# A fused perceiver layer: the order of the attention units, the place of the state-space stage, and silu written with exp and ln

## The chip, the cores and the metric

The kernel runs on one core of a Trainium2 chip. The metric is the device time of one execution in microseconds. Engines are named as in the profile: PE is TensorE, ACT is ScalarE, DVE is VectorE, POOL is GpSimd, SP is SyncE, whose queue issues nearly all DMAs.

## The reference

Inputs are 512 query rows `x` and 8192 context rows `ctx`, each of width 512. All arithmetic is float32. Three blocks follow one another, each added to `x`:

```
q, k, v = LN(x) Wq + bq, ctx Wk + bk, ctx Wv + bv        # 16 heads of 64
x += softmax(q k^T / 8) v Wo + bo                        # cross-attention

h = LN(x); r = rms(h) * norm1
xin, z = split(r in_proj^T)                              # 1024 channels each
xin = silu(causal_conv4(xin) + conv_b)
dt, B, C = split(xin x_proj^T)                           # 32, 16, 16
delta = softplus(dt dt_proj^T + dt_b)
s[t] = exp(delta[t] A) * s[t-1] + delta[t] xin[t] B[t]   # 16 states per channel
y = (sum over states s C + xin D) * silu(z)
u = h + y out_proj^T
x += u + (silu(rms(u) w1) * (rms(u) w3)) w2

h = LN(x); top 2 of 16 experts, sigmoid gates
x += gated experts(h) + shared expert(h)                 # silu(gate) * up, down
```

The recurrence runs over the 512 rows in order, so the second 256 rows need the states that the first 256 leave, and nothing of the first 256 depends on the second after attention.

## The kernel before

Every float32 matmul operand is split into a float16 high and a float16 low part, and a product is made of three float16 matmuls. Attention works on pairs of heads (8 pairs, `p`) and on halves of the 512 queries (`h`). A unit is one pair and one half: 32 steps (`NSTEP`), each over 256 of the 8192 context rows.

A step's `scores` (L345) runs eight score matmuls of 256 columns (L359, L360) into two PSUM tiles. ACT then takes the exponential twice, in float32 (L367, two instructions) and in float16 (L369, two instructions); in every second step (`m % 2 == 1`) DVE casts instead (L371). DVE subtracts the two to get the low part (L372). `av` (L375) multiplies by the values one step later: eight matmuls of 130 columns (value low, a zero, value high, a one, L389) and eight of 65 (L392), into one bank for each head of the pair. `unit_end` (L393) divides by the sums, transposes, adds the bias and stores a high and a low part in `oT` (L414, L415).

The maxima, keys and values come from `filler` (L421), a generator of PE work. One pass projects keys and values of two pairs over 16 context chunks (L250 to L252, L274 to L276) and takes each query's maximum (`smax_units`, L297, L302, L310). There are four passes (`NPASS`). Keys and values go to DRAM (`k_d`, `v_d`); `main_load` (L333) brings 1.3 MB for every four steps back through SP. Queries are placed by `qplace` into one of four pairs of tiles, 6 DMAs per pair; the row of maxima (`maxrow_units`) is written into the same tile.

The order on PE is the program's own in attention (`manual_schedule`); all other orders are a planner's. Units run pair by pair, both halves of a pair in turn:

```python
units = [(p, h) for p in range(NPAIR) for h in range(2)]      # L543
NFILL = 12 * NSTEP - 4                                        # L560
rate = (NPASS - 1) * PASSN / NFILL                            # L561
```

Pass 0 runs by itself; passes 1 to 3 are spread evenly over the first 12 units by `advance`, twice in each step. `weight_prep` (L509) splits the later weights, one yield in every second step. Units 12 to 14 have no filler. Unit 15 (loop at L605) takes two yields of `tail` per step: the output projection of the first 256 rows (`wo_proj(0)`), `prep(0)` and `delta(0, 0)`.

`tail` (L630) holds the rest. `prep(s)` (L764) does norms, in-projection, convolution, silu (ACT's Silu, L795, L796), x-projection, and broadcasts B and C from DRAM to 128 partitions (`load_bc`, L856). `delta(s, q)` (L866) makes softplus and `silu(z)` (L890) for two of eight channel blocks. `scan(s, b)` (L896) goes through four chunks of four states: four exponentials on ACT (L906), a product (L909), the scan (L913) and a product (L916) on DVE, and sums over states on PE with the identity as weight (L919). Three buffers `dAs` and `hss` rotate. After attention a loop over eight (s, q) (L1050) runs the scans, with `prep(1)` between those of the first half, and `outproj(0)` and the MLP of the first half (`ffn`, L952) between those of the second. `lnexp` (L655) loads the ACT table that holds exp and ln after each Silu. Then come `outproj(1)`, the MLP of the second half, router, shared expert and 18 expert rounds (`moe`, L1256).

Of the kernel before, what the change touches and what calls it, by code (L numbers as in the profile page):

```python
# [37 lines left out]
def perceiver_layer(ctx: ExitStack, tc: tile.TileContext, a: dict, out: bass.AP):  # L38
# [8 lines left out]
    oT = const.tile([P, 2, NPAIR, NQ], F16, name="oT", tag="big16")  # L47
    oTh, oTl = oT[:, 0], oT[:, 1]
# [5 lines left out]
    ]  # L54
    k_d = [[scr.tile([P, 2, 2 * CH], F16, name=f"k_d{p}_{c}") for c in range(NDC)] for p in range(NPAIR)]
# [90 lines left out]
    NQT = 4  # L146
    qlms = []
    qhhs = [(L if i == (NPAIR - 1) % NQT else sb1).tile([P, 2, NQ], F16, name=f"qhh{i}") for i in range(NQT)]
    for i in range(NQT):
        t = (L if i == (NPAIR - 1) % NQT else sb1).tile([P, 2, NQ], F16, name=f"qlm{i}")  # L150
        nc.gpsimd.memset(t[64:128], 0.0)
        qlms.append(t)
# [60 lines left out]
    def qplace(p, qh, ql):  # L213
        qhh = qhhs[p % NQT]
        qlm = qlms[p % NQT]
        for hh in range(2):
            s = slice(hh * 64, hh * 64 + 64)
            nc.sync.dma_start(qhh[0:64, hh, :], qh[s])
            nc.sync.dma_start(qhh[64:128, hh, :], qh[s])
            nc.sync.dma_start(qlm[0:64, hh, :], ql[s])  # L220
        state[p]["q"] = qhh, qlm
# [91 lines left out]
    def maxrow_units(p, runm):  # L313
        qlm = state[p]["q"][1]
# [9 lines left out]
        for hh in range(2):  # L324
            nc.sync.dma_start(
                qlm[64:65, hh, :].rearrange("o (a b) -> o a b", b=P), r[hh * 4 : hh * 4 + 4, :]
            )
# [17 lines left out]
    def scores(u, m, ld, sp, alone=False):  # L345
# [3 lines left out]
        qhh, qlm = state[p]["q"]  # L349
        qs = slice(h * HQ, (h + 1) * HQ)  # L350
        pss = []
        for i in range(2):
# [5 lines left out]
            for hh in range(2):  # L358
                nc.tensor.matmul(ps[:, hh], lhsT=k[:, hh, sl], rhs=qhh[:, hh, qs], start=True, stop=False)  # L359
                nc.tensor.matmul(ps[:, hh], lhsT=b[:, hh, sl], rhs=qlm[:, hh, qs], start=False, stop=True)  # L360
# [4 lines left out]
        cast = m % 2 == 1  # L365
# [9 lines left out]
    def av(po, m, x):  # L375

        v, ph, pl = x
        kw = dict(skip_group_check=True)
        for x in range(2):
# [14 lines left out]
    def unit_end(u, po, sp):  # L394
        p, h = u
        oq = sp.tile([P, 2, 2, 64], F32, name="oq", tag="oq", bufs=1)
        rl = sp.tile([P, 2, 2], F32, name="rl", tag="rl", bufs=1)
        for hh in range(2):
            nc.scalar.copy(oq[:, :, hh, :], po[hh][:, :, 0:64])
        for hh in range(2):  # L400
            nc.vector.reciprocal(rl[:, hh], po[hh][:, :, VW - 1])
            nc.vector.tensor_tensor(oq[:, :, hh, :], po[hh][:, :, 65:129], oq[:, :, hh, :], ALU.add)  # L402
        for hh in range(2):
            nc.vector.tensor_tensor(
                oq[:, :, hh, :], oq[:, :, hh, :], rl[:, hh].unsqueeze(2).to_broadcast((P, 2, 64)), ALU.mult
            )
# [5 lines left out]
        qs = slice(h * HQ, (h + 1) * HQ)  # L412
        ptf = pt.rearrange("d q n -> d (q n)")
        nc.scalar.activation(oTh[:, p, qs], ptf, AF.Identity, bias=bv)  # L414
        nc.vector.scalar_tensor_tensor(oTl[:, p, qs], ptf, bv, oTh[:, p, qs], ALU.add, ALU.subtract)  # L415
# [5 lines left out]
    def filler():  # L421
# [22 lines left out]
        mr, nw = [], None  # L444
        for g in range(NPASS):
# [8 lines left out]
            else:  # L454
                wk, wv, wq = nw
                qh = [qproj(p, w) for p, w in zip(pr, wq)]
                yield 2 * 2592
            runm = [sb2.tile([P, 4, 2, CH], F16, name=f"runm{i}", tag=f"runm{i}", bufs=1) for i in range(2)] if g else None
            ks = [[None] * NCH for _ in pr]
            for c in range(NCH):  # L460
# [11 lines left out]
                for n, gen in enumerate(gens):  # L472
# [5 lines left out]
                    if mr and c == 0:  # L478
                        yield from mr.pop(0)
# [29 lines left out]
    def weight_prep():  # L509
# [10 lines left out]
        def fetch(j):  # L520
            f = sb2.tile([P, 1024], F32, name="mpf", bufs=2)
# [3 lines left out]
        nf = fetch(0)  # L525
        yield
        for j, (name, i, dst) in enumerate(blocks):
            f = nf
            if j + 1 < len(blocks):
                nf = fetch(j + 1)  # L530
# [44 lines left out]
    for n in range(NLAST * NSTEP):  # L575
        u, m = units[n // NSTEP], n % NSTEP
        if m == 0:
            assert state[u[0]].get("ready"), u
# [780 lines left out]
```

## Time and profile before

| what | value |
|---|---|
| median of 3 runs | 2650.54 us (2645.51 to 2652.3) |
| the profiled execution | 2653.45 us, span 2651.7 us |
| PE, DVE, ACT busy | 2410.6, 2049.4, 1955.5 us (91, 77, 74% of the span) |
| first step of units 0, 12, 13, 14, 15 | 278.5, 1650.9, 1703.1, 1755.2, 1809.8 us |
| last AV matmul of attention | 1914 us |
| first and last scan (L913) | 1918, 2263 us |
| first expert's matmul (L1222) | 2449 us |
| DMA | 531 MB, mean 200 GB/s |

The page cuts the span in 40 slices of 66 us; each digit is the busy share of a slice in tenths:

```profile
PE   7999998999999899998999998998878688998895
DVE  6876688877877877777877777997899999633785
ACT  5787787888787788867788887997868476432784
```

Slices 5 to 25 are attention beside the passes, 26 to 29 attention alone and with the preparation, 30 to 34 the scans, then MLP and experts. A duration in the profile includes latency that overlaps the next instruction, so the distance between starts is what an engine gives for one instruction. PE durations are modelled.

### The profile page before, as it was taken

Reading aid. Unit: us, or ns where it says so; the run is one execution under the profiler, and the core shown is the slowest. Engines: PE = TensorE matmul, PEld = TensorE weight load, DVE = VectorE, ACT = ScalarE, POOL = GpSimd, SP = SyncE. Lnnn points to the kernel's source line nnn. Section 1 sums busy time; section 2 is a strip of 40 time slices with the busy share of each in tenths; the row PEclk is TensorE's granted clock in tenths of the full one; section 3 lists DMA queues with packets and bytes.
Section 4 is the critical chain, followed back from the end, with each engine's and each line's share of the span. In section 5 each row is a group of like instructions: output and inputs, shape, how many; then the busy total and the mean of one; then the engine's idle time right before and its main releaser. Section 6 shows DMA issues by size and latency. Waiting matters only on the chain. (4 is left out here: it accounts for less than half of the span.)

```text
span 2651.7 us, 54346 instructions
## 1 busy us (share of the span) xinstructions
PE 2410.6 (91%) x21806; PEld 1693.5 (64%) x21806; DVE 2049.4 (77%) x2403; ACT 1955.5 (74%) x3734; POOL 44.2 (2%) x58
## 2 busy tenths in 40 slices
PE   7999998999999899998999998998878688998895
PEld 4454676777666677766677766997656466665442
DVE  6876688877877877777877777997899999633785
ACT  5787787888787788867788887997868476432784
POOL 2000000000000000000000000000000000001001
PEclk9999999999899999989999998999989889999998
DMA  7973899866598866658966655887511322675896
GB/s 265 308 255 128 268 284 270 242 169 187 166 268 264 265 189 176 184 152 250 253 176 190 173 162 129 201 204 206 171 56 41 96 72 82 229 233 200 294 337 222
DMA packets 353686, 531.42 MB, mean 200 GB/s; under 512 B 25106, under 2 KB 218834, under 8 KB 353300
## 3 DMA queue, kind: packets, MB, share of 16 engines
q1 hardware_dynamic: 352148, 523.69, 65.6%
q0 software_dynamic: 1280, 4.20, 0.5%
q8 instruction: 173, 2.83, 0.5%
q14 instruction: 85, 0.70, 0.1%
HBM read 397.68 MB, written 126.94 MB: 198 GB/s over the span
## 5 line engine op out<-in xcount | busy, mean ns | idle before, releaser
L372 DVE TENSOR_TENSOR phl<-p,phl 128x1024 f16<-128x1024 f32 x512 | 625.9, 1224 | 175.0 <-ACT phl L369 158.9
L367 ACT ACTIVATE p<-pss 128x512 f32<-128x512 f32 x1024 | 596.8, 619 | 126.1 <-PE pss L360 50.7
L302 ACT ACTIVATE sf<-psx 128x512 f16<-128x512 f32 x1024 | 557.7, 622 | 79.1 <-PE psx L297 77.2
L359 PE MATMUL pss<-qhh,k 128*128 128x256 f16 x2048 | 486.2, 277 | 18.5 <-ACT phl L369 18.0
L360 PE MATMUL pss<-qlm,kb 128*128 128x256 f16 x2048 | 485.2, 276 | 0.6 <-DMA kb<-k_d 0.4
L389 PE MATMUL po<-v,phl 128*128 128x130 f16 x4096 | 327.2, 222 | 5.2 <-DVE oq L402 4.7
L310 DVE TENSOR_TENSOR runm<-runm,sf 128x2048 f16<-128x2048 f16 x240 | 292.4, 1218 | 45.7 <-ACT sf L302 45.2
L389 PEld LDWEIGHTS <-phl 128*128 128x128 f16 x4096 | 273.9, 99 | 69.4 <-issue 21.5
L369 ACT ACTIVATE phl<-pss 128x512 f16<-128x512 f32 x512 | 312.3, 610 | 0.0
L274 PE MATMUL psv<-wh_v,ctxc 128*128 128x256 f16 x1024 | 283.4, 277 | 7.7 <-DVE khl L258 3.4
L275 PE MATMUL psv<-wl_v,ctxc 128*128 128x256 f16 x1024 | 282.2, 276 | 1.2 <-DVE wl_v L176 1.2
L276 PE MATMUL psv<-wh_v,ctxc 128*128 128x256 f16 x1024 | 282.1, 276 | 0.0
L359 PEld LDWEIGHTS <-k 128*128 128x128 f16 x2048 | 202.2, 99 | 63.7 <-issue 18.0
L360 PEld LDWEIGHTS <-kb 128*128 128x128 f16 x2048 | 202.7, 99 | 61.0 <-issue 22.2
L297 PE MATMUL psx<-khl,qh 64*128 64x512 f16 x1024 | 212.5, 395 | 21.3 <-ACT sf L302 18.4
L371 DVE CAST phl<-p 128x1024 f16<-128x1024 f32 x256 | 176.1, 688 | 58.1 <-ACT p L367 57.7
L392 PE MATMUL po<-v,phl 128*128 128x65 f16 x4096 | 209.9, 194 | 9.3 <-DVE phl L372 9.3
L250 PE MATMUL psk<-ctxc,wh_k 128*128 128x512 f16 x512 | 198.6, 388 | 21.1 <-DVE vs L281 10.5
L919 PE MATMUL py<-hs,ident 128*128 128x256 f32 x512 | 148.1, 447 | 67.1 <-DVE hs L916 67.0
L251 PE MATMUL psk<-ctxc,wh_k 128*128 128x512 f16 x512 | 197.2, 385 | 0.7 <-DVE ctxc L234 0.7
L252 PE MATMUL psk<-ctxc,wl_k 128*128 128x512 f16 x512 | 196.8, 384 | 0.0
L392 PEld LDWEIGHTS <-phl 128*128 128x128 f16 x4096 | 172.8, 98 | 12.8 <-DVE phl L372 12.0
(304 smaller groups left out, 3711.9 us busy)
## 6 DMA issues: line engine op xcount, KB each, us to landing
v<-v_d SPq DMA_DIRECT2D x128, 520.0 KB, 4.4
k<-k_d SPq DMA_DIRECT2D x256, 256.0 KB, 5.8
ctxc<-ctx_d SPq DMA_DIRECT2D x96, 512.0 KB, 5.2
wef<-in_gu_dram SPq DMA_DIRECT2D x72, 512.0 KB, 5.9
v_d<-vs SPq DMA_DIRECT2D x128, 260.0 KB, 3.8
k_d<-khl SPq DMA_DIRECT2D x128, 256.0 KB, 4.2
kb<-k_d SPq DMA_DIRECT2D x128, 256.0 KB, 5.4
wpm<-w_d SPq DMA_DIRECT2D x48, 512.0 KB, 3.9
```

The costliest lines, as they stand in the source:

```text
L274: nc.tensor.matmul(ps[:, t, :], lhsT=ct[i // 2][:, 0, i % 2, sl], rhs=wh[:, i, :], start=i == 0, stop=False)
L275: nc.tensor.matmul(ps[:, t, :], lhsT=ct[i // 2][:, 0, i % 2, sl], rhs=wl[:, i, :], start=False, stop=False)
L276: nc.tensor.matmul(ps[:, t, :], lhsT=ct[i // 2][:, 1, i % 2, sl], rhs=wh[:, i, :], start=False, stop=i == NC4 - 1)
L302: nc.scalar.activation(dst, ps, AF.Copy, scale=1.0 / (8.0 * WS))
L310: nc.vector.tensor_tensor(r, r, sf, ALU.max)
L359: nc.tensor.matmul(ps[:, hh], lhsT=k[:, hh, sl], rhs=qhh[:, hh, qs], start=True, stop=False)
L360: nc.tensor.matmul(ps[:, hh], lhsT=b[:, hh, sl], rhs=qlm[:, hh, qs], start=False, stop=True)
L367: nc.scalar.activation(p32[:, i], pss[i], AF.Exp, scale=sc)
L369: nc.scalar.activation(ph[:, i], pss[i], AF.Exp, scale=sc)
L372: nc.vector.tensor_tensor(pl, p32, ph, ALU.subtract)
L389: nc.tensor.matmul(o, lhsT=ph[:, i, hh, qs], rhs=vv, start=first, stop=False, **kw)
L392: nc.tensor.matmul(o, lhsT=pl[:, i, hh, qs], rhs=vv_, start=False, stop=last, **kw)
```

## The change

1. Units go through all eight pairs with the first half of the queries, then through all with the second. The three later passes lie beside the first 6 units (192 steps, `NPREP`), and `weight_prep` advances at every step with a third load buffer. Queries go to DRAM (`q_d`), together with the row of maxima, and `qload` brings a unit's half in three DMAs into one of two tile pairs, up to four steps ahead.
2. From step 192 (unit 6) on, all values of a unit go into one PSUM bank: `av` issues per head, tile and query block three matmuls of 65, 64 and 65 columns. The freed bank holds the output projection and `py`.
3. From step 194 on `tail` is advanced in the attention loop; it yields the number of steps until its next turn. The output projection takes each pair as its unit ends (`ended`); `prep(0)`, then `delta(0, q)` and `scan(0, b)` lie beside units 8 to 14. Two `dAs` and `hss` there, four later. A cast on DVE in every fourth step for units 8 to 15 (`casts`).
4. Silu outside the last stages is `x * exp(-ln(1 + exp(-x)))`: `sigmoid` gives three ACT passes, DVE multiplies. The MLP of the first half (`exps=True`) does so too.
5. After attention: `wo_proj(1)`, `prep(1)` with `outproj(0)` and two MLP blocks between, then delta and scans of the second half with an MLP block after each scan.

```diff
-    units = [(p, h) for p in range(NPAIR) for h in range(2)]
+    units = [(p, h) for h in range(2) for p in range(NPAIR)]
+    NPREP = 2 * (NPASS - 1) * NSTEP
-    NFILL = 12 * NSTEP - 4
+    NFILL = NPREP - 4
...
+    for n in range(NU * NSTEP):
+        j, m = n // NSTEP, n % NSTEP
...
+        if n == NPREP:
+            while pend:
+                drain()
+            finish()
...
+            half = tail(tc, a, out, const, scr, ident, x_sb, mlp_d, oTs, y_d, xd_d, (ps_s, ps_o, ps_x, bank_j), ended)
+            turn = n + 2
...
+        cur = scores(u, m, loads[n // 4], sp, n > NFILL, 2 if j < NPAIR else 4)
+        advance(start + LEAD + (n + 0.5) * rate)
+        if m == 4:
+            finish()
+        while half and n >= turn:
+            d = next(half)
+            if d is None:
+                turn = NU * NSTEP
+            else:
+                turn = max(turn, n) + d
...
+        if m >= NSTEP - 4 and j + 1 < NU:
+            p, h = units[j + 1]
+            if state[p].get("ready") and ("q", h) not in state[p]:
+                qload(j + 1, units[j + 1])

-        cast = m % 2 == 1
+        cast = m % casts == 1

+        if len(po) == 1:
...
+                        nc.tensor.matmul(o, lhsT=ph[:, i, hh, qs], rhs=vh1, start=first, stop=False, **kw)
+                        nc.tensor.matmul(o[:, 0:64], lhsT=ph[:, i, hh, qs], rhs=vl, start=False, stop=False, **kw)
+                        nc.tensor.matmul(o, lhsT=pl[:, i, hh, qs], rhs=vh1, start=False, stop=last, **kw)

+    def qload(j, u):
+        p, h = u
+        qs = slice(h * HQ, (h + 1) * HQ)
+        qhh, qlm = qts[j % 2]
+        nc.sync.dma_start(qhh[0:64], q_d[p][0:64, 0, :, qs])
+        nc.sync.dma_start(qhh[64:128], q_d[p][0:64, 0, :, qs])
+        nc.sync.dma_start(qlm[0:65], q_d[p][0:65, 1, :, qs])
+        state[p]["q", h] = qhh, qlm

+    def sigmoid(src, scale, bias=None):
+        t = m2.tile([P, 2, H], F32, name="sig", tag="w2k", bufs=4)
+        for j in range(2):
+            kw = {} if bias is None else dict(bias=bias[:, j : j + 1])
+            if bias is not None:
+                nc.scalar.activation(t[:, j], src[:, j], AF.Exp, scale=-scale, **kw)
+            elif j == 0:
+                nc.scalar.activation(t, src, AF.Exp, scale=-scale)
+        nc.scalar.activation(t, t, AF.Ln, bias=one)
+        nc.scalar.activation(t, t, AF.Exp, scale=-1.0)
+        return t

     def scan(s, b):
-            dlu[s, q].append(ps_s.tile([P, 2, H], F32, name="py", tag="pss"))
+            pp, tag = (ps_s, "pss") if s else (ps_o, "po1")
+            dlu[s, q].append(pp.tile([P, 2, H], F32, name="py", tag=tag))
...
+            yield 3
             for n in range(4):
                 k = nq * 4 + n
                 nc.tensor.matmul(py[:, j, :], lhsT=ident, rhs=hs[:, n, 1:], start=k == 0, stop=False)
+            if nq < 3:
+                yield 2

+    yield 44
+    yield from wo_proj(0)
+    yield from prep(0)
+    yT0 = None
+    for q in range(4):
+        yield from delta(0, q)
...
+        for j in range(2):
+            yield from scan(0, 2 * q + j)
+        gate(0, q, yT0)
+    yield None
```

The yields of `prep(0)` sum to 35 steps, of `delta` to 5, of `scan` to 20. In all, `tail` before attention's end takes steps 194 to 480 of 512.

## The prediction

> **What bounds the kernel now.** I read the page first: PE is busy for 91% of the span, DVE for 77%, ACT for 74%, an average over stages with different limits. So I cut the span where the step starts (every fourth score matmul, L359) and the first scan (L913) show a change of stage, and asked for the busy time of each engine in each stretch (columns: stretch and its length, then busy us and instructions of PE, PEld, DVE, ACT, POOL, the granted clock, DMA share, GB/s).
>
> ```profile
> 0.00:278.50 278.50, 254.71 (x1550) 135.34 (x1551) 197.44 (x231) 199.21 (x366) 19.50 (x25) 0.95 0.71 238
> 278.50:1650.90 1372.40, 1313.01 (x13410) 945.14 (x13409) 1059.96 (x1267) 1104.53 (x2160) 2.29 (x6) 0.97 0.73 210
> 1655.00:1808.00 153.00, 149.41 (x2259) 139.33 (x2258) 146.19 (x163) 144.13 (x290) 0.00 (x0) 1.00 0.82 203
> 1809.80:1914.00 104.20, 86.79 (x977) 71.01 (x974) 80.08 (x131) 83.73 (x164) 0.53 (x1) 0.95 0.69 196
> 1914.00:2080.00 166.00, 129.30 (x624) 96.48 (x625) 157.70 (x148) 116.86 (x278) 0.37 (x5) 0.90 0.15 48
> 2080.00:2270.00 190.00, 147.84 (x801) 111.03 (x799) 181.66 (x161) 107.95 (x227) 4.78 (x5) 0.93 0.27 85
> 2270.00:2452.00 182.00, 164.63 (x1201) 112.73 (x1199) 75.28 (x149) 64.15 (x88) 8.46 (x8) 0.95 0.69 235
> 2452.00:2651.70 199.70, 159.44 (x922) 77.64 (x920) 145.43 (x153) 130.61 (x159) 8.22 (x8) 0.94 0.80 284
> ```
>
> The rows are: pass 0; units 0 to 11 beside passes 1 to 3; units 12 to 14 alone; unit 15 beside the preparation of the first half; the scans of the first half; those of the second; the MLP with router and shared expert; the experts and the end. PE bounds rows 2 and 3 (96% and 98%), DVE bounds rows 5 and 6 (95% and 96%). In row 3 all three engines are nearly full, so attention has no engine to lend. In rows 5 and 6 PE is busy under 80% and ACT 60 to 70%.
>
> A busy time overlaps its neighbour's, so costs must come from starts. The timeline of PE in unit 13, columns start, length, what:
>
> ```profile
> 1732.32 0.27 PE L360 MATMUL pss<-qlm,kb 128*128 128x256 f16 x1
> 1732.42 0.62 PE L389 MATMUL po<-v,phl 128*128 128x130 f16 x8
> 1732.88 0.40 PE L392 MATMUL po<-v,phl 128*128 128x65 f16 x8
> 1733.13 0.27 PE L359 MATMUL pss<-qhh,k 128*128 128x256 f16 x1
> ```
>
> Eight 130-column matmuls take 0.46 us from start to start (57 ns each), eight of 65 columns 0.25 (30 each), a score matmul 109. A step is 8 x 109 + 8 x (57 + 30) ns = 1.57 us; units 12 and 13 took 52.2 and 52.1 us, 1.63 a step. The same view of ACT there, and of DVE in the scans:
>
> ```profile
> 1731.16 0.59 ACT L369 ACTIVATE phl<-pss 128x512 f16<-128x512 f32 x1
> 1731.63 0.60 ACT L367 ACTIVATE p<-pss 128x512 f32<-128x512 f32 x1
> 1732.11 0.62 ACT L369 ACTIVATE phl<-pss 128x512 f16<-128x512 f32 x1
> ```
>
> ```profile
> 1984.33 2.29 DVE L913 TENSOR_TENSOR_SCAN hs<-dA,hs 128x1028 f32<-128x1028 f32 x1
> 1986.54 1.20 DVE L909 TENSOR_TENSOR hs<-bc,du 128x1024 f32<-128x1024 f32 x1
> 1987.65 1.22 DVE L916 TENSOR_TENSOR hs<-hs,bc 128x1024 f32<-128x1024 f32 x1
> 1988.79 2.29 DVE L913 TENSOR_TENSOR_SCAN hs<-dA,hs 128x1028 f32<-128x1028 f32 x1
> ```
>
> So ACT needs 0.477 us per exponential of 512, DVE 2.21 per scan and 1.13 per product of 1024 (L372 has that size: 1.14); its cast L371 is 0.72 behind the next start. A step with a cast in every second one costs ACT 3 x 0.477 = 1.43, DVE 1.14 + 0.36 = 1.50.
>
> **The change part by part. Units 0 to 5 beside the passes.** The passes' work now lies beside 192 steps instead of 384. Row 2 is bound by PE, so the stage loses what 192 steps take on PE: 192 x 1.57 / 0.975 (granted clock) = 309 us; I take 307. The rest, 1065 us, is projections and maxima. ACT needs 768 evacuations of maxima x 0.478 + 192 of projections at some 0.53 + 192 x 1.43 = 744 of these 1065, DVE 192 maxima x 1.13 + 192 evacuations at 0.63 + 104 weight splits at 0.94 + 192 x 1.50 = 724. Neither comes near. Weight preparation runs at every step: its 52 loads and 104 stores stay hidden as now (DMA share 0.73; attention's loads of 1.3 MB per 4 steps are halved in number, so the rate stays at some 210 GB/s). The queries go through DRAM, three loads per unit on SP; the next unit's are issued up to four steps (20 us) ahead, so I cost them at nothing; uncovered, they cost a landing of about 5 us at each of 16 units. Unit 6 starts at 278.5 + 1065 = 1343.5.
>
> **Units 6 and 7.** Alone but for the first output projection, which takes 42 matmuls of 216 ns there = 9.1 us on a full PE, and the emptying of the pipeline at the pool change (unit 14 took 54.6 against 52.1): 104.3 + 9.1 + 2.5 = 116.
>
> The new AV order splits 130 columns into 65 + 64: 24 small matmuls per step for 8 + 8. A rule speaks against this: the Trainium skill, TensorE: Matmul & The Clock Gate, section Back-to-back issue gap, gives about 81 ns sustained for a stream of weight load and matmul pairs at 128 columns. By it 24 pairs cost 1.94 us, 1.25 more per step, 80 us in these two units alone. The row L392 is exactly such a stream, with a weight load before each, at 30 ns; by it the cost is 0.72 against 0.70. I take the row, from 0 to +0.1 us per step.
>
> **Units 8 to 15, the state-space part beside them.** The program spends 9 steps until the projection is done, 35 on the preparation, 4 x 45 on delta and scans, and 32 steps are left. With a cast in every fourth step, ACT costs (8 + 6) x 0.477 / 4 = 1.67 a step, DVE 1.14 + 0.18 = 1.32, PE 1.57.
> - 9 steps: 15 us.
> - Preparation. Added on DVE: convolution 32 instructions, 24 x 0.40 + 8 x 0.26 = 11.7; norms, gates and splits some 16. On ACT: per pair of blocks a copy 0.48, three halo and split copies 0.7, sigmoid 2 x 0.36 + 2 x 0.52; with the norms 20. On PE 14.8. ACT 58.4 + 20 = 78.5, DVE 74, PE 73: three nearly equal loads. Row 4 is the nearest: 104 us with 83.7 on its busiest by union. But it holds table loads that are removed (below). I take 85.
> - Scans, per 45 steps: DVE 45 x 1.32 + 8 chunks x 4.48 (a scan, two products) + 4.2 for delta and gate + 1.3 for unit ends = 100.8. ACT 75.2 + 14.2 (32 exponentials of 256 at 0.40, carries) + 4.8 + 0.5 = 94.7. PE 70.6 + 32 x 0.218 + 3.2 = 81, at the clock of row 5 some 88. So DVE bounds it: 403 for four. Row 5 ran at 95% of DVE: 403 / 0.96 = 420. Bounds: 403, and 485 at the 83% that row 4 made of PE.
> - 32 steps at 1.67: 53.5.
>
> Sum 15 + 85 + 420 + 53.5 = 573.5; attention's end at 1343.5 + 116 + 573.5 = 2033.
>
> Moved queues: the eight broadcast loads of 512 KB stand on SP ahead of the next chunk's k. At 284 GB/s (last row) 4.2 MB take 15 us against 9 for four steps: up to 6 us, once, inside the range. The store before them waits for ACT's xd, with those loads behind it; k is loaded a chunk ahead. POOL only clears tiles. The AV of a unit's first step waits for DVE's reading of the old sums, now behind a scan of 2.2 us; while DVE bounds the stage this costs nothing.
>
> **Silu by exp and ln.** Row 4's ACT groups and waits:
>
> ```profile
> L795 ACT ACT_TABLE_LOAD x2 | 2.6, 1283 | 0.0
> ...
> L367 ACT ACT_TABLE_LOAD x1 | 1.3, 1283 | 0.0
> ```
>
> ```profile
> PE pss L359 <- ACT phl L369: 10.6, 6, 4.3
> ```
>
> Eleven loads in that stretch, 14.1 us, and PE waits up to 4.3 us for ACT. The Trainium skill (ScalarE: Activation LUTs, What ACT_TABLE_LOAD costs) adds a drain of 1.38 us, 2.66 per switch. The row speaks against it: the next instruction starts 1.29 us after the load's start (median of L656). Kept beside attention, four gates with two switches each would cost ACT 10.3 us by the row, 21 by the rule. The new form costs two more passes of 0.52 each. In the later stages ACT is not the bound, and the saved loads are worth nothing.
>
> **After attention.** Now serial: projection 48 x 0.216 = 10.4; the second half's norms 14 (x_sb written at 1833.1, first transpose at 1847.1 in the first half), beside the 10.4 of the first output projection; then PE: transposes 2, in-projection 4 x 2.6, convolution 32 x 0.218 = 7, MLP of the first half 13, x-projection 2.6 = 35, 38 at clock 0.93; then store and broadcast 8, unit end 2: 72 us. Row 6 loses about 4 of DVE work: 186. The MLP row loses one up and two down blocks, 10.4 of PE, and keeps a little idle: 174. Last row unchanged: 199.7.
>
> Sum: 2033 + 72 + 186 + 174 + 199.7 = 2665 us of span, 13 more than 2651.7. The profiled execution itself took 2653.45 and the median of the three runs is 2650.54, so the prediction is 2650.5 + 13.5 = **2664**.
>
> The trade in short: row 5 (166) and the overlap of row 4 leave the end, and come back beside attention, because attention alone fills all three engines; the cast that ACT takes over gives DVE only 0.18 us of 1.50.
>
> **Rivals.**
> 1. *The queues mesh.* DVE full during scans (403), preparation at 78.5, passes packing tighter (-15, of row 2's 59 us without PE work), the chain after attention 60 and the scans behind it 175: -17 - 6.5 - 15 - 12 - 11 = 2602. For it: row 3 runs at 98% of its busiest with the others at 94. Against: row 5's DVE waits although it has nothing else to do. Faster; decided if the 45 steps take under 103 us.
> 2. *PE waits for the scan.* Its order is fixed: scores, then the identity matmuls of a chunk (L919 before), then AV. If one attention product and one scan product (2.3 us) still stand ahead on DVE when PE reaches a chunk, 32 x 2.3 = 74 us: 2738. For it: row 4 made 83% of PE. Against: three steps, 7 us, lie between issue and use. Decided at over 110 us per 45 steps.
> 3. *Small matmuls cost the rule's price*: over 2850. The row is against it.
> 4. *Nothing gained or lost*: the shares of 1 and the forecast cancel, 2650.
>
> **How the numbers follow.** Forecast 0.50, spread 2645 to 2690; rival 1: 0.24; rival 2: 0.19; rival 3: 0.03; rival 4: 0.04. Within 0.3% of before (2642.6 to 2658.5, about what a measurement of this kernel tells from no change) lie rival 4 and 0.11 of the forecast's spread: 0.15. Faster: rival 1 and the rim, 0.26. Slower: 0.59. The range 2605 to 2740 leaves a tenth out at each side.
>
> **What would show it.** Unit 6 at 1343 and a stage of 1065 before it; two units of 52 us plus the projection; DVE over 93% busy during the scans, steps of 2.3 us; AV starts at 30 ns; no table load before attention's end; the second half's first scan 72 us behind the last AV. Wrong would be: a first stage bound by ACT or by the px and pj banks with filler twice as dense, PE waits on the identity matmuls, or a slower AV stream.

## The result and the profile after

The changed kernel takes 2715.66 us (median of 4 runs, 2712.51 to 2716.54) against 2651.42 (2645.51 to 2652.36) before: the ratio is 1.0245, with an interval of 1.0227 to 1.0263. It is 64 us slower, where 13.5 were forecast. Its profiled execution took 2715.5 us with a span of 2713.8.

The page of the changed kernel, the three engines in 40 slices of 68 us:

```profile
PE   7999999999999999999799988888899888698995
DVE  6776687678876678666787898989886498732785
ACT  5787778877778867888787998888886645332784
```

PE is as full as before in nearly all slices up to 22. In slices 23 to 28, the scans beside attention, it shows 8, and DVE goes up and down between 8 and 9. The same stretches as in the prediction, cut where units 0 and 6 and steps 256 (unit 8), 300 and 480 start, then at the last AV, the first scan of the second half, and so on (columns as there: stretch, length, busy us and instructions of PE, PEld, DVE, ACT, POOL, granted clock, DMA share, GB/s):

```profile
279.80:1335.30 1055.50, 1014.08 (x8824) 648.42 (x8823) 771.35 (x945) 813.68 (x1568) 1.28 (x7) 0.97 0.69 213
1335.30:1460.00 124.70, 116.30 (x2045) 101.55 (x2044) 100.28 (x106) 103.98 (x205) 1.17 (x4) 0.99 0.82 205
1460.00:1565.20 105.20, 93.82 (x1554) 82.84 (x1551) 87.91 (x137) 93.05 (x199) 0.10 (x1) 0.97 0.67 173
1565.20:2015.50 450.30, 380.84 (x6151) 341.38 (x6148) 403.53 (x369) 393.19 (x843) 0.00 (x0) 0.98 0.59 149
2015.50:2076.20 60.70, 58.33 (x1090) 51.95 (x1087) 46.15 (x46) 58.70 (x123) 0.00 (x0) 1.00 0.58 146
2076.20:2160.30 84.10, 76.36 (x480) 54.26 (x477) 33.45 (x77) 39.55 (x96) 0.32 (x3) 0.94 0.42 137
2160.30:2336.00 175.70, 134.81 (x691) 100.06 (x688) 165.15 (x135) 85.39 (x206) 5.03 (x5) 0.89 0.27 88
2336.00:2511.50 175.50, 150.37 (x1076) 105.72 (x1076) 69.45 (x144) 52.72 (x76) 7.88 (x8) 0.91 0.62 212
2511.50:2713.80 202.30, 165.99 (x937) 80.44 (x936) 149.63 (x156) 133.15 (x162) 8.46 (x8) 0.93 0.81 284
```

Set beside the forecast:

| stage | forecast | measured |
|---|---|---|
| units 0 to 5 beside the passes | 1065 | 1055.5 |
| units 6, 7 | 116 | 124.7 |
| 9 steps, then preparation (35 steps) | 15 + 85 | 22.1 + 83.0 |
| scans of the first half, 4 x 45 steps | 420 | 450.3 |
| last 32 steps | 53.5 | 60.7 |
| last AV to the first scan of the second half | 72 | 84.1 |
| scans of the second half (first to last start) | 186 | 173.0 |
| then to the end | 174 + 199.7 | 178.2 + 202.3 |

Attention ends at 2076 in place of 1914, 162 us later; what follows takes 637.6 us in place of 737.7, 100 less. The difference is the 62 us of the two spans. The largest single error, 30 of the 49 us between forecast and measured span, is the fourth row: DVE's busy time is 403.5 us, as worked out, but it is 90% of the stage and not 96%.

That row is two stages in one. In each 45 steps the fourth to the 39th hold the chunks: all 96 of their DVE instructions (product, scan, product with C) and all 128 exponentials for dA fall into these 4 x 36 = 144 steps. The other nine of each 45 hold `delta`, `silu(z)`, the gate and the last identity matmuls. One stretch of nine steps and the 36 steps behind it:

```profile
1665.90:1685.60 19.70, 19.65 (x330) 18.06 (x327) 13.61 (x15) 17.57 (x36) 0.00 (x0) 1.00 0.59 144
1685.60:1777.30 91.70, 75.38 (x1217) 66.97 (x1214) 86.88 (x78) 80.56 (x175) 0.00 (x0) 0.98 0.56 141
```

The sums of the 144 steps with chunks and of the 36 without:

```profile
sum 369.90, PE 302.10 PEld 269.14 DVE 348.88 ACT 322.35 POOL 0.00; mean PE 75.52 PEld 67.28 DVE 87.22 ACT 80.59 POOL 0.00
...
sum 80.40, PE 78.75 PEld 72.24 DVE 54.65 ACT 70.85 POOL 0.00; mean PE 15.75 PEld 14.45 DVE 10.93 ACT 14.17 POOL 0.00
```

With chunks DVE is 94% busy and PE 82%; without them PE is 98% busy and DVE 68%. So DVE bounds the first kind, as it bounded row 5 before (95%), and PE the second. The distances between starts say the same of the nine steps shown: 72 score matmuls of 109 ns, 222 of the AV at 30, 26 more of 109 and 10 in float32 of 218 make 19.5 of the 19.7 us. Of DVE's 47 us of idle time 26 lie in the 36 steps.

What the engines wait for in the whole of that row (columns: engine, line, tile, what ended the wait; us in total, times, longest):

```profile
PEld L392 <- DVE phl L374: 53.8, 45, 2.7
PE po L392 <- DVE phl L374: 48.1, 41, 2.6
ACT p L369 <- PE pss L362: 36.1, 44, 1.9
DVE phl L374 <- ACT phl L371: 31.2, 34, 1.8
ACT carry L968 <- DVE hs L966: 8.9, 12, 2.0
...
PE py L976 <- DVE hs L969: 7.3, 3, 3.0
```

It is a ring: PE waits for DVE's low part (L374), ACT for PE's scores, DVE for ACT's exponentials. The timeline of DVE and then of PE there shows how one link arises:

```profile
1801.35 1.22 DVE L962 TENSOR_TENSOR hs<-bc,du 128x1024 f32<-128x1024 f32 x1
1802.48 0.68 DVE L373 CAST phl<-p 128x1024 f16<-128x1024 f32 x1
1803.08 0.68 DVE L942 SCALAR_TENSOR_TENSOR zs<-pz,sig 128x512 f32<-128x512 f32 x1
1803.68 1.21 DVE L374 TENSOR_TENSOR phl<-p,phl 128x1024 f16<-128x1024 f32 x1
```

```profile
1804.95 0.20 PE L392 MATMUL po<-v,phl 128*128 128x65 f16 x1 [1.50 <-DVE phl L374]
1804.99 0.20 PE L390 MATMUL po<-v,phl 128*128 128x65 f16 x1
1805.03 0.19 PE L391 MATMUL po<-v,phl 128*128 128x64 f16 x1
1805.05 0.19 PE L392 MATMUL po<-v,phl 128*128 128x65 f16 x1
```

The first matmul with the low part waits 1.50 us for the subtraction of 1803.68, ahead of which DVE did a chunk's product, a cast and the product of `silu(z)`; the next scores stand behind that matmul on PE. After the wait the stream runs at 0.02 to 0.04 us from start to start, so rival 3's 81 ns is out.

### The profile page after: what moved, and what is told of

It reads as the page before. It is cut to its first block, busy times and chain, and to the rows that moved or that the text cites. A ratio compares the mean times of both kernels' runs of the same rounds, so it can differ in the third digit from the quotient of the medians.

```text
span 2713.8 us, 59474 instructions
## 1 busy us (share of the span) xinstructions
PE 2444.0 (90%) x24366; PEld 1701.3 (63%) x24366; DVE 2025.8 (75%) x2342; ACT 1973.0 (73%) x3837; POOL 41.6 (2%) x58
## 5 line engine op out<-in xcount | busy, mean ns | idle before, releaser
L374 DVE TENSOR_TENSOR phl<-p,phl 128x1024 f16<-128x1024 f32 x512 | 619.8, 1221 | 174.7 <-ACT phl L371 168.7
L369 ACT ACTIVATE p<-pss 128x512 f32<-128x512 f32 x1024 | 611.4, 626 | 124.9 <-PE pss L362 98.9
L371 ACT ACTIVATE phl<-pss 128x512 f16<-128x512 f32 x640 | 404.2, 633 | 0.0
L392 PE MATMUL po<-v,phl 128*128 128x65 f16 x2560 | 270.8, 196 | 56.8 <-DVE phl L374 55.8
L390 PE MATMUL po<-v,phl 128*128 128x65 f16 x2560 | 279.4, 194 | 13.0 <-DVE oq L423 11.6
L392 PEld LDWEIGHTS <-phl 128*128 128x128 f16 x2560 | 237.9, 98 | 67.6 <-DVE phl L374 65.5
L391 PE MATMUL po<-v,phl 128*128 128x64 f16 x2560 | 278.8, 194 | 0.0
L390 PEld LDWEIGHTS <-phl 128*128 128x128 f16 x2560 | 240.5, 99 | 22.1 <-DVE oq L423 13.7
L301 PE MATMUL psx<-khl,qh 64*128 64x512 f16 x1024 | 228.6, 395 | 28.0 <-ACT sf L306 22.4
L391 PEld LDWEIGHTS <-phl 128*128 128x128 f16 x2560 | 240.1, 98 | 8.1 <-issue 0.8
```

The lines of the kernel that those rows point to most:

```text
L369: nc.scalar.activation(p32[:, i], pss[i], AF.Exp, scale=sc)
L371: nc.scalar.activation(ph[:, i], pss[i], AF.Exp, scale=sc)
L374: nc.vector.tensor_tensor(pl, p32, ph, ALU.subtract)
L390: nc.tensor.matmul(o, lhsT=ph[:, i, hh, qs], rhs=vh1, start=first, stop=False, **kw)
L391: nc.tensor.matmul(o[:, 0:64], lhsT=ph[:, i, hh, qs], rhs=vl, start=False, stop=False, **kw)
L392: nc.tensor.matmul(o, lhsT=pl[:, i, hh, qs], rhs=vh1, start=False, stop=last, **kw)
```

## Experiments

Theory W: the ring is opened by PE's wait for the low part. Rival E: three queues that are all 85 to 90% full, in orders fixed ahead, lose about a tenth to one another wherever the single wait shows (in the expectations of the first runs it is theory L). Neither divides the row as above; the table at the end of this section does that for the runs. Each run stands beside runs of the kernel before on the same chip; a ratio is to those. Lines of code shift by a few between the kernels.

**PE's wait for the low part.** In `e1_low_last` the sixteen matmuls with the high part come first (`for x in range(2):` around the loops, high at x = 0, low at x = 1). In `e2_lag2` the AV lies one step further behind:

```diff
-        while len(pend) > (2 if m == 2 else 1):
+        lag = 2 if n >= NPREP else 1
+        while len(pend) > (lag + 1 if m == 2 else lag):
```

`e3_both` has both.

> The same matmuls of the one-bank AV in another order: all 16 with the high part of the weights first, then the 8 with the low part, as the kernel before had it. Theory W (the changed kernel loses time because its third AV matmul already needs DVE's low part, 0.06 us behind the scores instead of 0.46 us and more; 48 us of such PE waits in the scan stage, about 4 us in unit 6): the steps of the mixed stage get shorter, 25 to 45 us off 2715, so 2670 to 2690, and PE's waits for L374 fall below 20 us. Rival theory L (the mixed stage is held by the load and the queue order of DVE and ACT; PE's wait only shows that lateness): 0 to 10 us off, 2705 to 2715, the waits move to the low-part matmuls in their new place.

> The AV order of the changed kernel, but from step 192 on AV runs two steps behind its scores instead of one, so that the low part has a whole step more. Theory W: the wait for L374 goes, 25 to 45 us off, 2670 to 2690, as in the run with the low part last. Theory L: 0 to 10 us off, 2705 to 2715, since DVE and ACT have the same work in the same order.

> Low part last and AV two steps behind, together. Theory W: no better than the better of the two alone, about 2670 to 2685. Theory L: as each alone, over 2700.

Measured: 2703.2 (1.0198, 1.0173 to 1.0223), 2723.56 (1.0275, 1.0249 to 1.0302) and 2716.53 (1.0238, 1.0221 to 1.0255). The scans took 443.5, 448.9 and 445.6 us. The scans of e2_lag2 and the waits in them:

```profile
1572.20:2021.10 448.90, 388.21 (x6152) 347.95 (x6149) 404.39 (x369) 391.77 (x842) 0.00 (x0) 0.94 0.62 149
```

```profile
DVE phl L374 <- ACT phl L371: 32.5, 35, 3.5
ACT p L369 <- PE pss L362: 24.9, 24, 3.8
...
PE po L390 <- DVE oq L423: 21.5, 5, 7.3
...
PE po L392 <- DVE phl L374: 12.0, 14, 2.2
```

The wait that W names falls from 48 to 12 us, and the stage keeps its length: DVE is idle as long as before, and PE now stands up to 7.3 us at the ends of units, where the one bank must be read before the next sums start. The granted clock was 0.94 there against 0.98, and PE was busy 7 us longer; that can hide a few us of a gain, not the 25 to 45 that W asked for. W as the main cause falls. The order of e1 is worth some 12 us, 7 of them in the scans, for half a microsecond (16 matmuls of 30 ns) more before each need.

**The casts and silu.** `e4_casts2` casts in every second step in all units; `e5_silu` takes ACT's Silu, with a table load each way, for `silu(z)` of the first half.

```diff
-        cur = scores(u, m, loads[n // 4], sp, n > NFILL, 2 if j < NPAIR else 4)
+        cur = scores(u, m, loads[n // 4], sp, n > NFILL, 2)
```

> One edit undone: a cast on DVE in every second step of units 8 to 15 too, instead of every fourth. Load per 45 steps of the scan stage: DVE 100.8 + 45 x 0.18 = 109, ACT 94.7 - 10.8 = 84. Theory L with DVE as the bound: 4 x 8 = 32 us longer in the scans, less 4 us in the last unit, which ACT bounds: 2735 to 2745. Theory W: a DVE with more to do is later with the low part, but the low part also starts earlier, behind a shorter ACT: within 15 us of 2715.

> One edit undone: silu(z) of the first half, beside attention, by ACT's own Silu again (four gates, so eight table loads of 1.29 us, against two more passes of 0.52 us each; DVE has one multiplication of 0.6 us less per gate). Sum of loads: ACT +10.3 - 4.2 = +6 us, DVE -2.4. If the table loads only add load: 2713 to 2722. If, as in the stage of unit 15 before, PE waits out each burst with nothing to take its place: 10 us or more, 2725 to 2735.

Measured: 2721.87 (1.0265, 1.0247 to 1.0283) and 2721.17 (1.0263, 1.0237 to 1.0288). With the casts back DVE is busy 430 of the 455.9 us (94%) of the scans and ACT 353: 27 us more work on DVE, with 40 less on ACT, make the stage 6 us longer, where 32 were expected if DVE bounds it throughout. In the steps with chunks DVE is then busy 98% of the time, so it can be filled there. The trace of e5 shows three table loads per gate and not two, as an exponential of attention falls between (L942, L369, L681): twelve of 1.29 us, 15.5 us on ACT. They make the scans 7 us longer and the whole 5.5. Neither edit is a large cause either way.

**The order without the mixing.** `e6_order_only` runs all of `tail` after attention (`while half and n >= turn` becomes `while False`, and the generator is emptied after the loop). `e10_two_banks` is that with the two-bank AV in all units (`if True:` in `drain`), `e11_order_low_last` that with e1's order.

> Only the new order of the units: the whole first-half state-space part is taken out of the attention loop and runs after the last unit. Units 8 to 15 should then take 54 us each (1.67 us a step, ACT) against 616 us together in the changed kernel: 180 us less; behind them projection 10, norms 14, preparation some 45, delta 8, scans 4 x 40 / 0.96 = 168: 245 us more. So 2780, if mixing the stages is worth 65 us. If mixing is worth nothing because all three engines are full anyway: 2715.

> As the run with the new order of units but the first half's state-space part after attention (2783.6 us), with the two-bank AV of the kernel before in all units: eight matmuls of 130 columns and eight of 65 per step. Units 6 and 7 alone took 56.4 and 56.8 us in that run, units 12 and 13 of the kernel before 52.2. Theory A (the one-bank AV costs the 4.4 us per unit): units 6 and 7 take 52 to 53 us, units 8 to 15 some 1.67 to 1.70 a step in place of 1.75; time 2755 to 2775 us. Rival (the units are longer for another reason: the tiles of queries loaded through DRAM, the pool change or their place): units 6 and 7 stay at 56 to 57 us and the time within 5 us of 2783.

> As the run with the new order of units but the first half's state-space part after attention (2783.6 us), with the one-bank AV kept and only its order changed: the sixteen matmuls with the high part of the weights first, then the eight with the low part. Theory W (the 4.4 us per unit of the one-bank AV are the wait for the low part, which DVE delivers last and which the third matmul of each step needs): units 6 and 7 take 52.5 to 54 us, time 2758 to 2772 us. Rival (it is the price of 24 matmuls with 24 weight loads in place of 16): units 6 and 7 stay at 56 to 57 us, time 2778 to 2788 us.

Measured: 2783.56 (1.0496, 1.047 to 1.0522), 2785.18 (1.0488, 1.0459 to 1.0517), 2785.35 (1.0485, 1.0451 to 1.0519). The mixing is thus worth some 67 us to the changed kernel (by the ratios); the new order without it is slower than both kernels. The 2755 to 2775 us of e10's theory did not come. Attention alone in e6, units 6 and 7 and the 180 steps from step 300 on (the same columns as above), then the same two stretches of e10:

```profile
1334.60:1447.80 113.20, 108.10 (x2008) 98.03 (x2006) 99.21 (x106) 101.75 (x204) 1.13 (x4) 0.98 0.84 212
1525.90:1842.00 316.10, 307.98 (x5790) 279.50 (x5787) 249.06 (x249) 311.91 (x637) 0.00 (x0) 1.00 0.78 194
```

```profile
1335.10:1443.80 108.70, 103.92 (x1509) 94.66 (x1507) 99.28 (x109) 101.05 (x206) 1.18 (x4) 0.98 0.86 214
1521.20:1839.20 318.00, 301.90 (x4335) 270.45 (x4332) 250.42 (x261) 313.17 (x647) 0.00 (x0) 0.99 0.77 192
```

In units 6 and 7, with a cast in every second step, the one-bank AV costs 113.2 - 108.7 = 4.5 us, 0.07 a step. With a cast in every fourth step both forms take 316 to 318 us for 180 steps, 1.76 each, with ACT busy 98 to 99%: there ACT is the bound and the AV's form does not count. PE is 97% busy beside it in e6, so two nearly full queues need not lose a tenth. e11 is inconclusive: 53.6 us for unit 6, as its theory said, 58.5 for unit 7, more than its rival said.

**Which load paces the scans.** `e7_less_dve` leaves out the product with C in the first half's scans, `e8_less_act` 84 of its 128 exponentials for dA, `e16_less_both` both.

```diff
-            nc.vector.tensor_mul(hs[:, :, 1:], hs[:, :, 1:], BC[s][1, nq])
+            if s:
+                nc.vector.tensor_mul(hs[:, :, 1:], hs[:, :, 1:], BC[s][1, nq])
...
-                nc.scalar.activation(dA[:, n, 1:], dl[:, j], AF.Exp, scale=Av[:, b, k : k + 1])
+                if s or b == 0 or n == 0:
+                    nc.scalar.activation(dA[:, n, 1:], dl[:, j], AF.Exp, scale=Av[:, b, k : k + 1])
```

> Leaves out the product with C in the scans of the first half, so PE sums the bare states: 32 DVE instructions of 1.135 us, 36 us of DVE's load in the 450 us of the scan stage. If DVE is the bound there and its waits are incidental: 30 to 36 us off, 2680 to 2686. If the three queues are coupled, each at 84 to 90% and none the bound: only a part, 10 to 20 us, 2695 to 2706.

> Leaves out three of four exponentials of dA for seven of eight blocks of the first half (the values of the first block stay): 84 ACT instructions of 0.40 us, 34 us of ACT's load in the scan stage, nothing off DVE or PE. If DVE is the bound: within 5 us of 2715. If the queues are coupled: 10 to 20 us off, 2695 to 2706. If ACT is the bound: 30 us off, 2685.

> Both cuts at once, leaving out in the first half's scans the product with C (36 us of DVE) and 84 of the exponentials for dA (34 us of ACT). Alone they gave 20 and 2 us. Theory E (two nearly equal queues): the sum is more than the parts, since after the first cut ACT was the fuller engine: 45 steps in 95 to 102 us, time 2645 to 2675 us. If DVE's queue alone sets the pace: no more than the two together, 105 to 108 us per 45 steps, 2688 to 2695 us. If PE's own work sets it (85% busy): the same, 105 or more.

Measured: 2693.92 (1.0159, 1.0135 to 1.0183), 2713.11 (1.0219, 1.019 to 1.0248), 2699.71 (1.0184, 1.0147 to 1.022); the scans 432.0, 447.0 and 433.1 us. The scans of the three in the same order:

```profile
1561.60:1993.60 432.00, 378.79 (x6152) 340.33 (x6149) 371.48 (x337) 390.78 (x843) 0.00 (x0) 0.98 0.62 156
...
1568.80:2015.90 447.10, 378.59 (x6154) 340.29 (x6151) 403.09 (x369) 362.60 (x759) 0.00 (x0) 0.98 0.59 150
...
1567.50:2000.60 433.10, 375.85 (x6154) 338.53 (x6151) 371.88 (x337) 361.82 (x759) 0.00 (x0) 0.98 0.62 156
```

Taking 32 us from DVE (403.5 to 371.5 busy) shortens the stage by 18, all of it in the steps with chunks. The edit also takes a link out of the chain from the scan to the identity matmuls, so load and chain are not told apart. Taking 31 us from ACT gives 3 us alone and nothing after DVE's. My expectation that two equal queues hold each other, so that the two cuts together give more than their sum, fell: with 372 and 362 us of work DVE and ACT are 86 and 84% busy, and PE 87%, yet the stage gets no shorter.

**The order on DVE's queue.** The planner puts scan, products and subtractions in a row of its own making. `e14_manual` takes the program's order for DVE from step 194 to attention's end, with the product, the scan and the product with C in three successive steps:

```diff
             turn = n + 2
+            ms.enter_context(tc.manual_schedule(engines={mybir.EngineType.DVE}))
...
+            yield 1
             hf = hs.rearrange("p n t -> p (n t)")
...
+            yield 1
             nc.vector.tensor_mul(hs[:, :, 1:], hs[:, :, 1:], BC[s][1, nq])
...
-            yield 3
+            yield 1
```

`e15_manual_lag` adds the edits of e3. `e18_manual_spaced` is e14 with `yield 3` kept and the `yield 2` behind the identity matmuls left out; `e19_spaced_low_last` adds e1's order.

> Changed kernel; from step 194 to the end of attention the order on DVE is the program's, as PE's is, and the product, the scan and the product with C of a chunk are issued in three successive steps (the planner put a scan and one or two products in a row). So at most one state-space instruction, 2.2 us, stands ahead of a subtraction. Theory Q (runs of state-space work on DVE's queue make PE late, PE makes ACT late, and ACT makes DVE idle): PE's wait for the low part falls from 48 to under 25 us in the scans, the 45 steps take 103 to 107 us in place of 112.6, time 2680 to 2700 us. Theory E (DVE and ACT are within 3% of each other in load, 101 and 98 us per 45 steps, each waits for what the other has late, whatever the order): 110 to 113 us per 45 steps, time 2705 to 2718. It can be longer, up to 2740, if the fixed order puts a scan that waits for its exponentials ahead of a subtraction.

> As the run with DVE's order given by the program, and with the AV two steps behind from step 192 on and its sixteen matmuls with the high part first. Theory Q: PE no longer waits for the low part at all (under 5 us in the scans), and the stage goes to DVE's load: 102 to 106 us per 45 steps, 2675 to 2695 us. Theory E: no further gain over the run without the lag. In an earlier run the lag alone gave nothing, since PE then waited 21 us at unit ends for the bank of the old sums; that wait should stay small here because the division no longer stands behind several state-space instructions.

> As the run with DVE's order given by the program, and with the identity matmuls of a chunk three steps behind its product with C in place of one; the next chunk's product is issued in the same step, and a pair of blocks takes 49 steps in place of 45, so 16 steps without scans are left before attention's end in place of 32. From step 300 to the last AV the changed kernel takes 511 us. Theory Q (runs of state-space work on DVE's queue make PE late): neither wait is left, 465 to 490 us, time 2670 to 2695. Theory E (two nearly equal queues wait for each other in any order): 500 to 515 us, 2705 to 2720. If the wait on the product with C stays even so (over 50 us in sum), a fixed order in which the subtraction waits for ACT ahead of the state-space work is itself the loss: 2750 or more.

> As the run before it, with the sixteen AV matmuls of the high part first and the eight of the low part last. In the changed kernel that order was worth 12 us. Theory Q: little is left for it to gain, 0 to 5 us under the run before it. Theory E: again some 10 us under the run before it, since it gives PE 0.5 us more in every step until it needs the low part.

Measured: 2928.38 (1.1038, 1.1004 to 1.1073), 2940.55 (1.1089, 1.1056 to 1.1122), 2750.66 (1.0381, 1.0353 to 1.0409), 2735.8 (1.0322, 1.0294 to 1.035). Waits of e14_manual from 1620 to 2100 us, in its scans (L979 are the identity matmuls, L972 the product with C):

```profile
PE py L979 <- DVE hs L972: 133.5, 25, 7.4
DVE phl L374 <- ACT phl L371: 126.9, 43, 8.1
ACT p L369 <- PE pss L362: 116.2, 34, 7.4
...
PE po L392 <- DVE phl L374: 9.2, 4, 3.3
```

No expectation came near the first two times: the longest named for e14 was 2740. The wait for the low part is all but gone, and the ring is far wider elsewhere: this is the mechanism of rival 2, which the changed kernel has for 7 us only, since its planner issues the product early enough. With the identity matmuls two steps later (e18) that wait vanishes, and from 1566 to 2080 us the old one is back:

```profile
PE po L392 <- DVE phl L374: 49.7, 41, 2.9
DVE phl L374 <- ACT phl L371: 43.0, 45, 3.6
ACT carry L970 <- DVE hs L968: 31.4, 32, 1.8
ACT p L369 <- PE pss L362: 29.7, 35, 5.1
...
PE po L390 <- DVE oq L423: 22.5, 7, 7.1
```

From step 300 to the last AV e18 takes 524 us and e19 515, the changed kernel 511; 19 to 22 more are lost in the preparation, which is under the fixed order too. So theory Q of these runs, runs of state-space work in DVE's queue as the cause, fell. E's 500 to 515 us for e18 were missed too; e19's gain of 15 us over e18 is nearer to the 10 that E expected than to Q's 0 to 5. A fixed order that is better than the planner's is not excluded.

**Work moved to POOL.** `e9_pool` issues the product that fills a chunk (L962) on POOL in the first half's scans, `e12_before_pool` the same product (L909) in all scans of the kernel before; `e17_carry` moves the copy of the last states (L968) from ACT to POOL in the first half.

> Changed kernel with one edit: in the scans of the first half, beside attention, the product that fills a chunk (1024 elements, 1.13 us on DVE from start to start) is issued on POOL. POOL took about 1.22 us for 512 elements of float32 in the kernel before, so some 2.4 us for this product, 32 of them in the 450 us of the scans. Theory (DVE paces this stage, at 90% of its time, and work taken from DVE comes back at a bit over half, as when the product with C was left out: 20 of 36 us): scans 425 to 440 us, time 2690 to 2705 us. Rival 1 (the chain product, scan, product is longer by 1.3 us and the pair of chunk buffers does not cover that, so that PE waits at the identity matmuls): 2715 to 2740 us, with a PE wait on the scan's product. Rival 2 (POOL and DVE get in each other's way when both read float32 from SBUF: DVE instructions grow longer while POOL runs): over 2730 us, with DVE's start-to-start times longer than 1.13 and 2.21 us.

> Kernel before with one edit: in all scans the product that fills a chunk is issued on POOL in place of DVE. DVE is 95 and 96% busy in the two scan stages (166 and 190 us), POOL idle. Taken from DVE: 64 x 1.13 = 72 us. If POOL's product of 1024 elements takes some 2.4 us, POOL needs 2.4 of the 3.4 us that DVE then needs for a chunk, so it is not the bound; the rest of DVE's work is outside the scans and ACT needs 4 x 0.40 + 0.3 us a chunk. Theory (DVE bounds these stages, and POOL works beside it freely): 2585 to 2610 us. Rival 1 (with three buffers the longer chain of product, scan and product is not covered, the stage becomes a chain): 2620 to 2655 us. Rival 2 (both engines share the way to SBUF and DVE's instructions grow longer): 2650 us or more.

> Changed kernel; in the first half the copy of a chunk's last states (128 x 4), which stands on ACT and waits there for DVE's scan with the next exponentials behind it, goes to POOL. In the changed kernel's trace ACT waits 8.9 us for it in the scans, 12 times, up to 2.0 us. Theory H (ACT held behind the scan is what makes the stage long): 8 to 15 us less, 2700 to 2708 us. Theory E and theory Q: ACT has slack there (taking 34 us from it gave 2), so 0 to 4 us, 2711 to 2716 us. Longer than 2720 if POOL's short copies slow DVE as its products did.

Measured: 2753.06 (1.0378, 1.0352 to 1.0403), 2720.25 (1.0252, 1.0227 to 1.0277), 2730.31 (1.029, 1.0259 to 1.032). All are slower than the kernel that they edit. Groups of the kernel before in the 166 us of its first scans (columns: line, engine, operation, tiles, shapes, count; busy us, mean ns of one; idle before), and the same of e12_before_pool:

```profile
L913 DVE TENSOR_TENSOR_SCAN hs<-dA,hs 128x1028 f32<-128x1028 f32 x30 | 68.1, 2289 | 2.1 <-ACT dA L906 1.9
...
L916 DVE TENSOR_TENSOR hs<-hs,bc 128x1024 f32<-128x1024 f32 x28 | 33.6, 1215 | 1.1 <-ACT carry L915 1.1
```

```profile
L913 DVE TENSOR_TENSOR_SCAN hs<-dA,hs 128x1028 f32<-128x1028 f32 x26 | 74.8, 2892 | 11.7 <-ACT dA L906 9.0 <-POOL hs L909 2.6
L909 POOL TENSOR_TENSOR hs<-bc,du 128x1024 f32<-128x1024 f32 x24 | 73.3, 3075 | 87.9 <-PE py L919 47.1 <-ACT dA L906 15.9 <-DVE du L884 14.3
...
L916 DVE TENSOR_TENSOR hs<-hs,bc 128x1024 f32<-128x1024 f32 x25 | 42.6, 1718 | 1.2 <-ACT carry L915 1.2
```

DVE's scan grows from 2289 to 2892 ns and its product from 1215 to 1718, while POOL takes 3075 for what DVE did in 1214. In e9 the subtraction grew from 1217 to 1408 ns, 181 times, 35 us, nearly all that the move had freed (32 products of 1.13 us), and DVE's scan waited 13.5 us for POOL besides. In e17 DVE's times stay (1217 and 1219), but POOL's copy takes 744 ns against ACT's 232, the product with C waits for it now and then, and the planner's order is another; which of these makes its 15 us is not settled.

**The runs divided.** The 180 steps of the scans, cut in every run as in the changed kernel, us and DVE's busy share:

| run | 144 steps with chunks | 36 without |
|---|---|---|
| changed kernel | 369.9 (94%) | 80.4 (68%) |
| e1_low_last | 363.4 (96%) | 80.1 (68%) |
| e2_lag2 | 368.1 (94%) | 80.8 (73%) |
| e3_both | 364.9 (94%) | 80.7 (75%) |
| e4_casts2 | 376.1 (98%) | 79.8 (76%) |
| e5_silu | 376.9 (92%) | 80.6 (68%) |
| e7_less_dve | 351.4 (90%) | 80.6 (67%) |
| e8_less_act | 366.5 (95%) | 80.6 (68%) |
| e16_less_both | 352.4 (90%) | 80.7 (67%) |
| e9_pool | 407.4 (89%) | 80.5 (66%) |
| e17_carry | 384.1 (92%) | 80.6 (65%) |

The 36 steps take 80 to 81 us in all of them, with PE busy 97 to 98%. Most of the edits leave these steps alone; e1, e2 and e3 change the AV there and e4 gives DVE 6 us more and ACT 4 less, and the time stays. That is what a stretch bound by PE's work must show.

No version tried beats the kernel before; the best that computes all is e1_low_last, at 1.0198.

## Why the prediction was wrong in size

The sign held: the state-space part leaves the end and comes back beside attention, on engines that have little to lend, and the sum is a loss. The size did not: 2716 lies outside the forecast's own spread of 2645 to 2690. The chain of the forecast failed in these terms, with the difference to the measured time.

- *"So DVE bounds it: 403 for four. Row 5 ran at 95% of DVE: 403 / 0.96 = 420."* +30 us. The load was right to a microsecond. The step that failed is to sum it over all 180 steps and divide by one share, as if DVE bounded each of them. In the 144 steps with chunks it does, and 348.9 / 0.96 = 363 us stand against 369.9 measured: 6.5 of the 30. In the 36 steps without chunks PE is busy for 2.2 us a step and DVE for 1.5, and DVE's idle time there is not made up later: the sum gave them 54.65 / 0.96 = 57 us, they took 80.4. That is 23.5 of the 30. The prediction had PE's work (81 us per 45 steps), but not where it lies. The 0.96 is also row 6's share; row 5's own 0.95 makes 424.
- *"With a cast in every fourth step, ACT costs (8 + 6) x 0.477 / 4 = 1.67 a step."* +7 us in the last 32 steps. e6 shows 1.75 to 1.76 a step at 99% of ACT, and 59.6 us from step 480 to its last AV with nothing beside them. The 28 exponentials of eight steps are 13.4 us of 14.1; the rest is not assigned.
- *Units 6 and 7*, +8.7. Without the projection they take 113.2 (e6) where 106.8 were forecast; 4.5 of that is the new AV, for which I took nothing and bounded 0.1 a step, right in the bound; 2 stay open. The projection took 11.5, not 9.1.
- *9 steps, 15 us*: +7. The same steps take 16.4 in e6 with nothing beside them; the end of the projection was left out, six matmuls for which PE waits 2.6 us. The rest of the 5.7 is not assigned.
- *Last AV to the first scan, 72 us*: +12, and the second half's scans -13. The two terms cancel, because they were cut at different places: row 6 begins 12 us ahead of its first scan. Their sum, 258 us, was right to a microsecond.
- *First stage, 1065*: -9.5. Twice as much filler per step beside attention cost nothing. The rows show why: nothing but PE was near its limit there (DVE 73% and ACT 77% busy).
- *Silu by exp and ln* at nothing in the later stages and 10.3 us of ACT's time, less two passes, beside attention: e5 gives 5.5 us of the whole, with twelve table loads in place of eight.

The rivals do not name the first term. Rival 2 gave over 110 us per 45 steps as its mark, and 112.6 came, but by another way: PE's wait at the identity matmuls, its mechanism, cost 7 us and not 74. Of the signs named ahead, the stage before unit 6 and the AV starts of 30 ns came; DVE at 90% in place of over 93, 2.5 us a step in place of 2.3, and the table loads at 280 and 1341 us did not fit. Row 4 was misread in one place: by union its busiest engine is PE with 86.8 us, not ACT with 83.7.

What keeps DVE at 90% in the scans is shown for the larger part: the 36 steps that PE bounds. Rival E, that three nearly full queues lose a tenth whatever they do, does not stand: in row 3 before, PE, DVE and ACT were 98, 96 and 94% busy at once, and in the steps with chunks DVE loses 6%, about as much as in row 5. Two things stay open. No run spreads the chunks over all 45 steps; at 94 to 95% of DVE that would make 425 to 429 us of the 450, an estimate from 403.5 us. And no run shows what holds the steps with chunks when DVE's load is cut: there DVE is 90% busy in e7 and e16, ACT 91 and 83%, PE 85 and 84%. The waits for the low part (e2) and at the identity matmuls (e18) were taken away singly without a gain in the stage; ACT's for PE and DVE's for ACT were not.

## What to carry to other kernels

A load summed over a stage may be divided by one busy share only if the same engine bounds every part of it. Ask for each step what each engine has to do; where another engine bounds some of them, add those apart. Here that was 23.5 of the 49 us, and the busy share of the whole (90%) looked like queues holding each other up. When engines wait for each other in a ring, the wait that the profile lists first can be a symptom: take it away in one run, and see whether the stage gets shorter, before building on it. Forecast the order that comes out of removing a wait too: in e2 and e14 the next wait was there at once.

## What the runs showed of the hardware

POOL beside DVE is not free. The product of 1024 float32 elements that takes DVE 1.21 us takes POOL 2.9 to 3.1, and DVE's instructions with two inputs get longer: 16% in the mean of e9's subtractions, 26 and 41% for scan and product in e12 (spans on POOL are rough). The Trainium skill (SBUF — State Buffer, Who interferes with whom) says that a DVE instruction with two SBUF inputs contends with a GpSimd instruction that reads SBUF, and calls the contention an exclusive lock; the longer records agree in kind, and the runs do not show whether one waits for the other in full or both slow down.

Matmul streams of 64 and 65 columns, each with its own weight load, ran at 28 to 34 ns from start to start in the changed kernel (medians by the lines that follow one another), for 24 such pairs in a row.
